# A four-layer graph network: tile 1's products ahead of tile 2's transposes where one layer hands its rows to the next, with the residuals' buffers first, divisions kept in order and the denominators' transfers later

## Chip, cores and metric

The kernel runs on one core of a Trainium2 chip as one program. The metric is the device time in microseconds (us), as the median of several runs. A core has five engines that work side by side, each through its own instructions in order: PE (matrix products and transposes), DVE (vector work), ACT (scalar functions, copies), POOL and SP (here mostly issuers of DMA transfers). They meet through semaphores.

## What is computed

There are 3327 nodes with 512 features. Four layers follow each other, and each is wrapped in a residual and a row-wise layer norm. The reference, cut to its form:

```
x = layernorm(x + attention8(x, adj, W0, a0))            # layer 0, 8 heads of 64
x = layernorm(x + sage(x, adj, Wn, bn, Wl, bl, 64))      # layer 1, the "maps"
x = layernorm(x + elu(attention8(x, adj, W2, a2)))       # layer 2
x = layernorm(x + elu(attention4(x, adj, W3, a3)))       # layer 3, 4 heads of 128

attention: Wh = x @ W
           e[i,j] = leaky_relu(s1[i] + s2[j], 0.2), masked by adj
           out[i] = sum_j softmax_j(e[i,j]) * Wh[j]
sage:      keep the first 64 neighbours of each row (by a running count)
           xj = leaky_relu(mean over kept X @ Wn.T + bn)
           xi = leaky_relu(X @ Wl.T + bl)
           out = xi + xj where a row has a neighbour
```

## The kernel before

Rows lie in 26 tiles of 128 (`NT` = 26, the last one padded). The 0/1 adjacency stays on the chip as one fp8 `mask`. An attention runs over two halves of 13 row tiles, and in each over four slots of heads. Per tile of neighbours DVE makes weights `t` (L405), PE multiplies them with the values (`po`, L428), ACT makes the fp8 part `y` of the denominators (L408), and PE sums it (`pd`, L380). At the end of a slot the sums `po` are copied to `ob`, transposed by PE, copied to `hb` by ACT (L465) and stored to the DRAM array `hd` by SP (L466). The denominators of the last slot of the second half go another way: DVE transposes `pd` (L497, L501), reduces it to `red` (L505), SP stores `dd` (L507), and 16 small loads (L517) bring it back as `pes` in the right places (`place`). `finish_sums` (L532 to L538) turns `pes` into the reciprocals `rec`. Both are left over in `self.late`, for the next layer to call.

**Finishing rows.** The layer after an attention reads `hd` again and finishes it two tiles at a time with `finish_steps`: `load` fetches the tile `h` from `hd` and its residual `xr` from the previous layer's input (L126; `xr` on POOL's queue, `h` on SP's, or on POOL's for the first pair), `divide` multiplies by `rec` (L181) and, where the layer has an ELU, takes an exponential `e` on ACT (L186), `add` adds the residual (L197, or L194 and L195), and `norm_rows` takes statistics (L152, L153), a square root on ACT (L154), a reciprocal (L155, L158) and scales the row on ACT (L161). The first two tiles, 0 and 1, are finished inside the end of the attention itself.

**The two passages.** Two places do so while PE takes the finished tiles into products:

- *The maps* (`sage`, layer 0 to layer 1). `step1` transposes a tile on PE (`pt`, L724) and copies it to `xT` on ACT (L726). `step2` multiplies it with two 512 x 512 weights on PE (`pz`, L732, and `pi`, L735; 16 matmuls with their weight loads), and ACT and DVE split `pz` into bf16 parts and finish `pi` with the bias and the row (L736 to L746). SP stores two results (L742, L747).
- *The third projection* (`third`, layer 2 to layer 3). `project1` transposes (L261, L262, and a row sum L263), `project2` multiplies (`pw`, L271) and makes the values `vt` (L272 to L277). SP stores the finished tile (L133) and the values (L283).

In both loops a tile's products are put off by one tile: in each turn the transposes of the new tile come first, then the products of the pending one:

```
for s, y in enumerate(ys):
    xT = step1(y)
    if s == 0 and t0 + 2 < NT:
        ahead = finish(...)          # the pair after this one
    if pend:
        step2(*pend)
    pend = (y, xT, t0 + s)
```

**What sets the order.** PE's order is the program's (`manual_schedule` for PE). All other engines' instructions, and the DMA issues on their queues, are ordered by a planner at build time, by program order among what it expects to be ready, with its own estimate of times. `keep_in_program_order(ins)` holds one instruction behind everything written earlier for its engine. A buffer that is used again waits for its last reader. A pool opened after another has closed lies on the same memory, and waits for the last use of those bytes; within a pool, buffers are laid out in the order in which their names are first asked for. Before the change the pool of the maps' rows holds 6 buffers of `h` and after them 2 of `xr`; that of the third projection 10 of `h` and 6 of `xr`.

Of the kernel before, what the change touches and what calls it, by code (L numbers as in the profile page):

```python
# [7 lines left out]
F32 = mybir.dt.float32  # L8
# [5 lines left out]
ALU = mybir.AluOpType  # L14
# [4 lines left out]
P = 128  # L19
# [13 lines left out]
def kernel(  # L33
# [10 lines left out]
    nc = tc.nc  # L44
    N, F = x.shape
# [66 lines left out]
    rec = const.tile([P, NT, 8], F32, name="rec")  # L112
# [52 lines left out]
    def finish_steps(pool, xin, layer, t0, n, hbufs=6, eng=nc.sync, xbufs=None, xpool=None, ebufs=None, pinned=False):  # L165
        H, D = layer.H, layer.D
        ys, xs, steps = [], [], []

        def load():
            for t in range(t0, t0 + n):  # L170
                h = pool.tile([P, F], F32, name="h", bufs=hbufs)
                load_tile(h, hd, t, eng)
                ys.append(h)
                xr = xpool.tile([P, F], F32, name="xr", tag="hb") if xpool else \
                    pool.tile([P, F], F32, name="xr", bufs=xbufs)
                load_tile(xr, xin, t, nc.gpsimd)
                xs.append(xr)

        def divide(s):
            h = ys[s]  # L180
            nc.vector.tensor_tensor(h.rearrange("p (h d) -> p h d", h=H), h.rearrange("p (h d) -> p h d", h=H),  # L181
                                    rec[:, t0 + s, :H].rearrange("p (h e) -> p h e", e=1).to_broadcast([P, H, D]),
                                    op=ALU.mult)
            if layer.elu:
                e = pool.tile([P, F], F32, name="e", bufs=ebufs)
                ins = nc.scalar.activation(e, h, AF.Exp)  # L186
                if pinned and s == 0:
                    tc.keep_in_program_order(ins)
                xs.append(e)

        def add(s):
            h, xr = ys[s], xs[s]
            if layer.elu:
                nc.vector.scalar_tensor_tensor(xr, xs[n + s], 1.0, xr, op0=ALU.min, op1=ALU.add)  # L194
                nc.vector.scalar_tensor_tensor(h, h, 0.0, xr, op0=ALU.max, op1=ALU.add)  # L195
            else:
                nc.vector.tensor_tensor(h, h, xr, op=ALU.add)  # L197

        steps.append(load)
        for s in range(n):  # L200
            steps += [lambda s=s: divide(s), lambda s=s: add(s)]
        steps.append(lambda: norm_rows(pool, ys, t0))
        return ys, steps

    def finish(*a):
        ys, steps = finish_steps(*a)
        for f in steps:
            f()
        return ys
# [476 lines left out]
    def sage(first, first_pool, xin, prev, nxt, wsrc, dst):  # L686
# [3 lines left out]
        with tc.tile_pool(name="sg_z", bufs=1, reuse_waits="tile") as zp, \  # L690
# [21 lines left out]
            with tc.tile_pool(name="sa_w", bufs=1, reuse_waits="tile") as wp, \  # L712
                    tc.tile_pool(name="sa", bufs=2, reuse_waits="tile") as fp, \
                    tc.tile_pool(name="sa_t", bufs=2, reuse_waits="tile") as sp, \
                    tc.tile_pool(name="sa_ps", bufs=2, space=PSUM, reuse_waits="tile") as ps:
                wn = load_w(wp, wnT, "wn", nc.gpsimd)
                wl = load_w(wp, wlT, "wl", nc.gpsimd)
                blb = wp.tile([P, F], F32, name="blb")
                nc.gpsimd.dma_start(out=blb, in_=bl.to_broadcast([P, F]))

                def step1(xt):
                    pt = ps.tile([P, FC, P], F32, name="pt")
                    for c in range(FC):
                        nc.tensor.transpose(pt[:, c, :], xt[:, c * P:(c + 1) * P], ident)  # L724
                    xT = sp.tile([P, FC, P], F32, name="xT")
                    nc.scalar.copy(xT, pt)  # L726
                    return xT

                def step2(xt, xT, t):
                    pz = ps.tile([P, F], F32, name="pz")  # L730
                    for c in range(FC):
                        nc.tensor.matmul(pz, xT[:, c, :], wn[:, c, :], start=c == 0, stop=c == FC - 1)  # L732
                    pi = ps.tile([P, F], F32, name="pi")
                    for c in range(FC):
                        nc.tensor.matmul(pi, xT[:, c, :], wl[:, c, :], start=c == 0, stop=c == FC - 1)  # L735
# [12 lines left out]


                cr = fp.tile([NT, P], BF, name="cr", bufs=1)  # L750
                nc.sync.dma_start(out=cr, in_=ctd[NT:NT + 1, :].rearrange("o (t p) -> (o t) p", p=P))
                cnt = zp.tile([P, 3, NT], F32, name="cnt")
                pend = None
                ahead = first
                for t0 in range(0, NT, 2):
                    ys = ahead
                    if t0 in (4, 8):
                        prev.late.pop(0)(fp)
                    if t0 == 8:
                        cf = fp.tile([NT, P], F32, name="cf", bufs=1)  # L760
                        nc.scalar.copy(cf, cr)
                        pt = ps.tile([P, FC, P], F32, name="pt")
                        cb = pt[:, 0, :NT]
                        nc.tensor.transpose(cb, cf, ident[:NT, :NT])
                        nc.vector.tensor_scalar(cnt[:, 0, :], cb, NEIGHBOURS, 1.0, op0=ALU.min, op1=ALU.max)
                        nc.vector.reciprocal(cnt[:, 1, :], cnt[:, 0, :])
                        nc.vector.tensor_scalar(cnt[:, 2, :], cb, 0.0, None, op0=ALU.is_gt)
                    for s, y in enumerate(ys):
                        xT = step1(y)
                        if s == 0 and t0 + 2 < NT:  # L770
                            ahead = finish(fp, xin, prev, t0 + 2, 2, 6, nc.sync if t0 else nc.gpsimd)
                        if pend:
                            step2(*pend)
                        pend = (y, xT, t0 + s)
                step2(*pend)
            first_pool.close()

            with tc.tile_pool(name="sb_w", bufs=1, reuse_waits="tile") as wp, \
# [8 lines left out]
                wsb = wp.tile([P, FC, 2, FW + nxt.H], F32, name="wsb")  # L787
# [104 lines left out]
    def third(first):  # L892
        with tc.tile_pool(name="col3", bufs=1) as cp, tc.tile_pool(name="at_r3", bufs=2, reuse_waits="tile") as rp:
# [3 lines left out]
            with tc.tile_pool(name="p_w", bufs=1, reuse_waits="tile") as wp, \  # L897
# [3 lines left out]
                wsb = wp.tile([P, FC, 2, FW + L3.H], F32, name="wsb")  # L901
# [5 lines left out]
                pend = None  # L907
                ahead = first
# [12 lines left out]
                for t0 in range(0, NT, 2):  # L921
                    ys = ahead
                    if t0 in (4, 8):
                        L2.late.pop(0)(fp)
                    load_group(t0 + 6)
                    for s, y in enumerate(ys):
                        t = t0 + s
                        store_tile(x3, y, t, nc.sync)
                        xT = L3.project1(pp, ps, y, t)
                        if s == 0 and groups:  # L930
                            ahead, steps = groups.pop(0)
                            for f in steps:
                                f()
                        if pend:
                            L3.project2(pp, bank, wsb, *pend)
                        pend = (xT, t)
                        if t == HALF + 1:
                            L3.prepare(pp, 0)
                            L3.first_rows = L3.rows(rp, 0, 0)
                            L3.cut(pp, 0)  # L940
                L3.project2(pp, bank, wsb, *pend)
                L3.mean(pp, bank, wsb)

# [133 lines left out]
    with tc.tile_pool(name="col0", bufs=1) as cp, tc.tile_pool(name="raw", bufs=2) as rawp, \  # L1077
# [4 lines left out]
        with tc.tile_pool(name="p_w", bufs=1, reuse_waits="tile") as wp, \  # L1082
# [37 lines left out]
            wsb = wp.tile([P, FC, 2, FW + L0.H], F32, name="wsb")  # L1120
# [104 lines left out]
```

## Time and profile before

| what | us |
|---|---|
| median of 3 runs | 3393.33 (3391.39 to 3394.57) |
| the profiled run's own time | 3389.15 |
| its span, first to last instruction | 3387.4 |
| PE busy | 3251.2 (96%) |
| DVE busy | 2687.5 (79%) |
| ACT busy | 2354.6 (70%) |
| mean PE clock granted | 0.985 |
| chain of waits: share of PE | 85% |
| passage into the maps | about 950 to 1170 |
| passage into the third projection | about 2544 to 2690 |

Times in the profile are microseconds from the span's start. A timeline line gives start, length, engine, the line of the kernel, operation, `output<-inputs`, the shape and in square brackets the idle time of that engine just before, with what ended it. A line of the waits gives who waited for whom, the total, how often, and the longest. "issue" stands where the profile shows no releaser. `SPq` and `POOLq` are the queues' own instructions.

### The profile page before, as it was taken

To read this page: it belongs to the slowest core of one execution; us is meant where nothing else is said; L and a number is where in the kernel's file an instruction comes from. 1 tells how busy PE (TensorE), PEld (TensorE's weight loads), DVE (VectorE), ACT (ScalarE), POOL (GpSimd) and SP (SyncE) were. 2 spreads that over 40 slices of the span, in tenths; PEclk is the share of its full clock that TensorE was granted. 3 is DMA by queue.
4 is the path that set the end of the run, shared out by engine and by line. 5 is a ranking of instruction groups with operands and counts; after the bars stand their busy time and mean duration, and the time that the engine had idled before them with its cause. 6 is when DMAs were issued, how large, how long until landed. Compare 5 with 4: busy or idle time off the path is not lost.

```text
span 3387.4 us, 47182 instructions
## 1 busy us (share of the span) xinstructions
PE 3251.2 (96%) x18476; PEld 1626.4 (48%) x18476; DVE 2687.5 (79%) x2619; ACT 2354.6 (70%) x2143; POOL 239.8 (7%) x389
## 2 busy tenths in 40 slices
PE   8899999999979999999989999999998999999997
PEld 7634344444434445545544444444446754455453
DVE  5799999999967544444449999999998766668887
ACT  2398998999953333333338999999997655558986
POOL 3100000000010011111110000000002000010110
PEclk9999999999999999999999999999998999999998
DMA  9644111110143343333320111111117411122211
GB/s 368 222 124 127 49 49 38 55 49 28 44 123 125 122 117 84 91 85 87 80 77 20 47 48 50 51 48 47 35 31 241 152 41 42 41 51 80 94 42 49
DMA packets 288014, 284.29 MB, mean 84 GB/s; under 512 B 107492, under 2 KB 223534, under 8 KB 287791
## 3 DMA queue, kind: packets, MB, share of 16 engines
q1 hardware_dynamic: 254063, 170.62, 16.6%
q0 software_dynamic: 28208, 102.96, 9.5%
q10 hardware_dynamic: 5520, 7.69, 0.7%
q8 instruction: 146, 2.39, 0.3%
q14 instruction: 77, 0.63, 0.1%
HBM read 212.01 MB, written 69.17 MB: 83 GB/s over the span
## 4 chain that ended last, share of the span: by engine, by line
PE 85%; DVE 5%; DMA 4%; ACT 3%; issue 2%; SPq 0%; ACTq 0%; DVEq 0%; POOL 0%; POOLq 0%
PE po L428 52%; PE acc L859 12%; PE pd L380 7%; PE pw L271 5%; DVE t L405 3%; PE pz L732 3%; DMA raw<-in_adjT_dram 3%; PE pi L735 3%; ACT y L408 1%; PE pt L456 1%; PE pk L819 1%; DMA h<-hd 0%; PE pa L1108 0%; PE pt L724 0%; PE pct L664 0%
## 5 line engine op out<-in xcount | busy, mean ns | idle before, releaser
L405 DVE SCALAR_TENSOR_TENSOR t<-rb,qc,mask 128x1664 f32<-128x1664 f32 x1040 | 1960.3, 1954 | 169.4 <-PE po L428 147.3
L408 ACT ACTIVATE y<-t,bi,sc 128x1664 fp8e4<-128x1664 f32 x1040 | 1769.5, 1766 | 310.4 <-PE pd L380 292.7
L428 PE MATMUL po<-t,vj 128*64 128x448 f32 (+3 forms) x8320 | 1909.6, 521 | 22.1 <-DVE t L405 19.6
L428 PEld LDWEIGHTS po<-t,vj 128*64 128x64 f32 (+1 forms) x8320 | 838.9, 148 | 970.6 <-issue 704.0
L859 PE MATMUL acc<-zs,kt 128*128 128x512 bf16 x1352 | 401.1, 380 | 0.0
L271 PE MATMUL pw<-wsb,xT 128*128 128x264 f32 (+1 forms) x1248 | 302.2, 397 | 15.2 <-DVE vt L277 12.0
L859 PEld LDWEIGHTS <-kt 128*128 128x128 fp8e4 x2002 | 196.1, 98 | 242.1 <-issue 7.7
L811 ACT CAST pk<-cy 128x512 f32<-128x512 bf16 x169 | 99.0, 588 | 277.4 <-DVE kt L823 266.3
L271 PEld LDWEIGHTS pw<-wsb,xT 128*128 128x128 f32 x1248 | 241.1, 197 | 60.7 <-ACT xT L262 10.8
L380 PE MATMUL pd<-y,sden 128*32 128x448 fp8e4 (+1 forms) x4160 | 259.5, 342 | 10.4 <-ACT y L408 10.4
L859 PE MATMUL acc<-zl,kt 128*128 128x512 bf16 x650 | 246.5, 379 | 0.0
L380 PEld LDWEIGHTS <-sden 128*32 128x32 bf16 x4160 | 117.5, 96 | 162.5 <-issue 139.8
L823 DVE SCALAR_TENSOR_TENSOR kt<-pk,mask 128x512 fp8e4<-128x512 f32 x169 | 116.1, 688 | 94.0 <-PE pk L819 94.0
L277 DVE TENSOR_TENSOR vt<-pw,dc 128x256 f32<-128x256 f32 x156 | 59.0, 418 | 148.2 <-ACT dc L272 143.7
L359 POOL DMA_DIRECT2D rb<-r x40 | 21.3, 532 | 1670.4 <-DVE t L405 1652.2
L275 ACT COPY rc<-pw 128x8 f32<-128x8 f32 (+1 forms) x78 | 12.6, 162 | 156.6 <-PE pw L271 154.1
L831 DVE SCALAR_TENSOR_TENSOR y<-acc,cnt,bnb 128x512 f32<-128x512 f32 x26 | 19.5, 751 | 97.7 <-PE acc L859 90.3
L732 PE MATMUL pz<-wn,xT 128*128 128x512 f32 x208 | 94.9, 600 | 1.7 <-ACT xT L726 1.7
L700 POOL DMA_DIRECT2D cy<-ctd x91 | 67.9, 746 | 385.1 <-ACT pk L811 312.6
L735 PE MATMUL pi<-wl,xT 128*128 128x512 f32 x208 | 93.5, 592 | 0.0
L634 DVE TENSOR_SCALAR mask<-raw 128x832 fp8e4<-128x832 int32 (+2 forms) x90 | 54.8, 614 | 38.9 <-DMA raw<-in_adjT_dram 38.5
L154 ACT ACT_TABLE_LOAD x45 | 57.7, 1283 | 37.0 <-DVE mv L153 36.4
(187 smaller groups left out, 1699.3 us busy)
## 6 DMA issues: line engine op xcount, KB each, us to landing
vj<-v SPq DMA_DIRECT2D x312, 128.0 KB
rb<-r POOLq DMA_DIRECT2D x40, 832.0 KB, 4.8
raw<-in_adjT_dram SPq DMA_DIRECT2D x67, 416.0 KB
cy<-ctd POOLq DMA_DIRECT2D x78, 256.0 KB, 4.0
h<-hd SPq DMA_DIRECT2D x61, 256.0 KB
v<-vt SPq DMA_DIRECT2D x50, 256.0 KB
hd<-hb SPq DMA_DIRECT2D x48, 256.0 KB
xr<-x POOLq DMA_DIRECT2D x45, 256.0 KB, 3.1
```

The costliest lines, as they stand in the source:

```text
L271: nc.tensor.matmul(pw[e][:, :FW + H], xT[:, c, :], wsb[:, c, e, :], start=c == 0, stop=c == FC - 1)
L277: nc.vector.tensor_tensor(vt[:, hs, :], pw[e][:, :FW].rearrange("p (h d) -> p h d", d=D), self.dc[:, t, hs].rearrange("p (h e) -> p h e", e=1)
L380: nc.tensor.matmul(pd[c][32 * kk:32 * kk + 32, :w_], lhsT, rhs, start=(kk, c) not in seen, skip_group_check=final is not None, stop=last a ...
L405: nc.vector.scalar_tensor_tensor(t, rb[k], self.qc[:, j, h:h + 1], mask[:, j, i0:i0 + IW], op0=ALU.max, op1=ALU.mult)
L408: nc.scalar.activation(y, t, AF.Sigmoid, bias=self.bi[:, j, h:h + 1], scale=self.sc[:, j, h:h + 1], saturate=False)
L428: nc.tensor.matmul(po[c][k * D:(k + 1) * D, :z - a_], vj[:, j % 2, k * D:(k + 1) * D], ts[k][:, a_:z], start=j == 0, stop=j == NT - 1)
L700: nc.gpsimd.dma_start(out=cy[:, :n, :], in_=ctd[t:t + n, b * GW:(b + 1) * GW] .rearrange("(o t) i -> o t i", o=1).to_broadcast([P, n, GW]))
L732: nc.tensor.matmul(pz, xT[:, c, :], wn[:, c, :], start=c == 0, stop=c == FC - 1)
L735: nc.tensor.matmul(pi, xT[:, c, :], wl[:, c, :], start=c == 0, stop=c == FC - 1)
L811: nc.scalar.copy(pks[k % 2], carry[b, t // 4 * 4][:, t % 4:t % 4 + 2, :])
L823: nc.vector.scalar_tensor_tensor(kt, pk, NEIGHBOURS, mask[:, t:t + 2, i0:i0 + GW], op0=ALU.is_le, op1=ALU.mult, saturate=False)
L859: nc.tensor.matmul(acc, kts[t][:, s * P:(s + 1) * P], zs(t, c) if c < 2 else zl[:, t, :], start=t == 0 and c == 0, stop=t == NT - 1 and c ...
```

## The change

Five edits are made.

1. In both passages the products of tile 1 are issued at the end of the first turn (`t0 == 0`), before the transposes of tile 2. From tile 2 on the lag of one tile is as before.
2. `finish_steps` asks for `xr` before `h`, so that in a pool that is new the residuals' buffers lie in front. The order of the loads stays.
3. With `pinned`, the divisions of all tiles of a pair are written ahead of the additions, and divisions of pairs after tile 2 are kept in program order. The maps now pass `pinned` for the pairs at tiles 2, 4 and 6; the third projection passes it, as before, for tile 2 alone.
4. The pinned exponential is named more narrowly: layer 2, pair at tile 2, first tile.
5. In the maps the two left-over steps of the denominators (`place`, `finish_sums`) come at `t0` 6 and 10 in place of 4 and 8.

```diff
@@ finish_steps
         def load():
             for t in range(t0, t0 + n):
+                xr = xpool.tile([P, F], F32, name="xr", tag="hb") if xpool else \
+                    pool.tile([P, F], F32, name="xr", bufs=xbufs)
                 h = pool.tile([P, F], F32, name="h", bufs=hbufs)
                 load_tile(h, hd, t, eng)
                 ys.append(h)
-                xr = xpool.tile([P, F], F32, name="xr", tag="hb") if xpool else \
-                    pool.tile([P, F], F32, name="xr", bufs=xbufs)
                 load_tile(xr, xin, t, nc.gpsimd)
                 xs.append(xr)
 
         def divide(s):
             h = ys[s]
-            nc.vector.tensor_tensor(...)
+            ins = nc.vector.tensor_tensor(...)
+            if pinned and t0 > 2:
+                tc.keep_in_program_order(ins)
             if layer.elu:
                 e = pool.tile([P, F], F32, name="e", bufs=ebufs)
                 ins = nc.scalar.activation(e, h, AF.Exp)
-                if pinned and s == 0:
+                if pinned and layer.li == 2 and (t0, s) == (2, 0):
                     tc.keep_in_program_order(ins)
                 xs.append(e)
...
         steps.append(load)
-        for s in range(n):
-            steps += [lambda s=s: divide(s), lambda s=s: add(s)]
+        if pinned:
+            steps += [lambda s=s: divide(s) for s in range(n)] + [lambda s=s: add(s) for s in range(n)]
+        else:
+            for s in range(n):
+                steps += [lambda s=s: divide(s), lambda s=s: add(s)]
@@ sage (the maps)
-                    if t0 in (4, 8):
+                    if t0 in (6, 10):
                         prev.late.pop(0)(fp)
...
                         if s == 0 and t0 + 2 < NT:
-                            ahead = finish(fp, xin, prev, t0 + 2, 2, 6, nc.sync if t0 else nc.gpsimd)
+                            ahead = finish(fp, xin, prev, t0 + 2, 2, 6, nc.sync if t0 else nc.gpsimd, None, None, None,
+                                           t0 < 6)
                         if pend:
                             step2(*pend)
                         pend = (y, xT, t0 + s)
+                    if t0 == 0:
+                        step2(*pend)
+                        pend = None
                 step2(*pend)
@@ third (the third projection)
                             L3.cut(pp, 0)
+                    if t0 == 0:
+                        L3.project2(pp, bank, wsb, *pend)
+                        pend = None
                 L3.project2(pp, bank, wsb, *pend)
```

More of the change, by code (lines that the diff above doesn't have):

```diff
@@ L180, in divide @@
             h = ys[s]
-            nc.vector.tensor_tensor(h.rearrange("p (h d) -> p h d", h=H), h.rearrange("p (h d) -> p h d", h=H),
-                                    rec[:, t0 + s, :H].rearrange("p (h e) -> p h e", e=1).to_broadcast([P, H, D]),
-                                    op=ALU.mult)
+            ins = nc.vector.tensor_tensor(h.rearrange("p (h d) -> p h d", h=H), h.rearrange("p (h d) -> p h d", h=H),
+                                          rec[:, t0 + s, :H].rearrange("p (h e) -> p h e", e=1).to_broadcast([P, H, D]),
+                                          op=ALU.mult)
+            if pinned and t0 > 2:
+                tc.keep_in_program_order(ins)
             if layer.elu:
```

## Prediction

> **What bounds the kernel now.** I read the page first (PE 96% busy, 85% of the chain), then the chain of waits, then waits and timeline where PE is not busy. The change touches two passages, in which an attention's end hands its rows to the next layer's matrix products: 950 to 1170 us (layer 0 to the maps) and 2544 to 2690 us (layer 2 to layer 3's projection). Chain of waits, first passage (start, length, what):
>
> ```profile
> 983.10 0.82 ACT h L161
> 983.97 1.11 PE pt L724 x4
> 985.08 4.62 PE pz L732 x8
> 989.70 3.43 PE pi L735 x8
> 993.13 0.44 PE pt L724 x4
> 993.57 3.44 PE pz L732 x8
> ...
> 1164.92 3.45 PE pi L735 x8
> ```
>
> From 983.97 on only PE is on the chain, a tile every 7.31 us (0.44 transposes, 6.87 products), until 1168.37; ahead of it stands ACT's normalising of tile 2. So this stage ends when it starts plus its PE work. The timeline shows the start:
>
> ```profile
> 959.26 0.55 POOL L126 DMA_DIRECT2D h<-hd  x1
> 967.63 0.69 DVE L181 TENSOR_TENSOR h<-h,rec 128x512 f32<-128x512 f32 x1 [5.85 <-DMA h<-hd]
> 969.73 0.54 POOL L126 DMA_DIRECT2D xr<-in_x_dram  x1 [9.92 <-issue]
> 972.85 0.69 DVE L197 TENSOR_TENSOR h<-h,xr 128x512 f32<-128x512 f32 x1 [4.53 <-DMA xr<-in_x_dram]
> 977.21 0.69 DVE L181 TENSOR_TENSOR h<-h,rec 128x512 f32<-128x512 f32 x1 [2.25 <-DMA h<-hd]
> 983.97 1.11 PE L724 MATMUL pt<-ident,h 128*128 128x128 f32 x4 [13.84 <-ACT h L161]
> ```
>
> PE ends tile 0's products at 970.13 and stands 13.84 us with tile 1's xT ready: its order puts tile 2's transposes ahead of tile 1's products. Tile 2 is late because POOL stood 9.92 us before its residual xr, with tile 3's h and xr queued behind. In the compiled program before, that xr lies at byte 200,960 of a partition, over the last `hb` of the attention, whose store leaves SP near 962.8. DVE then held a division of tile 4 (977.21) ahead of tile 3's addition.
>
> Second passage, waits for 2565 to 2574 and busy times by stretch (length, PE, PEld, DVE, ACT, POOL, clock, DMA share, GB/s):
>
> ```profile
> PE pt L261 <- ACT h L161: 8.5, 1, 8.5
> ```
>
> ```profile
> 2565.00:2574.00 9.00, 0.54 (x4) 0.49 (x4) 8.97 (x21) 6.25 (x11) 2.35 (x5) 0.65 0.76 204
> 2574.00:2594.00 20.00, 20.00 (x92) 17.13 (x92) 18.16 (x42) 16.35 (x33) 3.06 (x6) 0.90 0.83 267
> 2594.00:2614.00 20.00, 19.02 (x96) 16.23 (x96) 18.49 (x44) 14.57 (x34) 1.77 (x4) 1.00 0.80 259
> 2614.00:2635.00 21.00, 16.06 (x85) 13.35 (x84) 20.07 (x60) 17.37 (x40) 2.69 (x5) 1.00 0.68 225
> 2635.00:2680.00 45.00, 45.00 (x224) 38.75 (x222) 31.70 (x79) 29.59 (x70) 1.06 (x2) 0.96 0.50 173
> ```
>
> The same wait, 8.46 us, but DVE is busy 65.7 of 70 us up to 2635: the supply of rows bounds this passage nearly as much as PE. I therefore price the two differently.
>
> **What the Trainium skill says.** "TensorE: Matmul & The Clock Gate", "What's actually happening": after an idle window of about 3.4 us the clock is halved until as much sustained work. The trace agrees: 1.11 and 4.62 us after the gap for 0.44 and 3.44. The same page, "Architectural detail": ACT and DVE are strictly first in, first out; DVE's wait at 977.21 fits. "DMA: Bandwidth & Descriptors", "Anatomy of one DMA": some 2.0 us fixed plus bytes / 436 GB/s, 2.6 us for 256 KB; the trace has 2.9 to 3.4 us alone and 8.3 us for tile 2's h behind the 1 MB `wl`. "ScalarE: Activation LUTs", "What ACT_TABLE_LOAD costs": 1283 ns, which the trace has too, and a drain of 1380 ns that it doesn't show: the square root starts at once after its load.
>
> **The change, part by part.**
>
> *Tile 1's products ahead (maps).* The 16 matmuls move from 985.08 to 970.13 and end at 977.0. Nothing is added. Tile 2's transposes, SP and POOL are not behind them in any queue; the five DVE operations (L738 to L746) and two ACT casts that follow move along.
>
> *Residuals in front (maps).* The two xr slots take the pool's lowest addresses: xr2 the very bytes of h2 before (188,672), into which its load went at once at 959.26, xr3 those of another `y` that PE last reads by 958.3. POOL then issues xr2, h3, xr3 at 959.8, 960.4, 960.9 (0.54 us each) instead of 969.7 to 970.8. They land behind `wl` (957.98 + 6.3 us) and h2 (967.6): at 250 to 324 GB/s about 1 us apiece, so xr3 near 971, an estimate. The new owner of byte 200,960 is tile 4's h, on SP: it can be issued from 969.7, before it was at 972.89. DVE does two divisions, two additions, two statistics for tiles 2 and 3 (0.69 us each) and two aggregates (0.17): done at 972.5 if nothing is between, at 976.0 if tile 0's five operations (3.45 us) are. From there to a normalised tile 2: square root 0.29, reciprocal 0.17, product 0.16, scaling 0.81 and gaps, 2.0 us; 3.4 us with DVE as busy as before. Tile 2 is ready between 974.5 and 979.4, PE at 977.0. Tile 3's scaling (0.7), xT's copy (0.6) and gaps (0.3) put the products of tile 2 between 977.9 (PE's own transposes) and 981.0. I take 979.2. From there 24 x 6.87 + 22 x 0.437 + 0.17 = 174.7 us, and 0.5 for tile 4: end 1154.4 against 1168.37, **14.0 us saved** (bounds 11.7 to 15.8). The clock's loss (0.67 + 1.18 us) is in it, as PE stands too briefly.
>
> *Divisions in order.* For tiles 4 to 7 of layer 0 they stay behind the DVE work written before, for tile 4 the last operation of tile 1 (PE 977.0, then 3 x 0.69: 979.3). Behind it wait tile 4's and 5's additions and statistics; tile 4 is ready 5.3 us on, 984.6, and PE wants it at 979.2 + 6.87 = 986.1. Tile 6's division stands behind tile 2's last operation, 988.2, ready 993.5, wanted near 1000.7. Cover: one product. If PE were early, 1 us (in the bounds).
>
> *Denominators later.* The 16 small DMAs (L517, near 0.61 us each on SP) and DVE's L532 to L538 (about 1.5 us) go two tiles' pairs back. On SP h4 to h7 pass ahead of 15 of them (before, six stood ahead of h4 and 15 of h6); behind them may come h8's load. That costs at most 16 x 0.61 = 9.8 us of queue near 1003, of which tile 8, wanted near 1015.3 and needing 3 us to land and 5.3 on DVE and ACT, feels 0 to 5.8: I take 0, as the load is free to go earlier (its slot is tile 2's, done at 988.2); 5.8 would make the forecast 3384.1, inside the range. Their reader is tile 13's division, two pairs of tiles on.
>
> *Second passage.* Tile 1's 16 products move to 2565.1 and end at 2569 to 2570.5. The wait for tile 2 (2573.5) is then 3 to 4.5 us; with the clock halved, tile 2's products begin near 2575.6 and end at 2581 against 2583.63. But tile 6 is ready at 2590.55 and was used at 2591.55: about 1 us of lead passes, and ACT's copies (0.98 us at 2601, 1.30 at 2618) and `rr` (3.64 at 2635) come next. The new layout here puts tile 3's h in the slot that held xr3: POOL's 1.1 us wait for PE moves one place up, h3 issues 1.6 us and the two `wsb` loads 0.55 us later; tile 3's division (2556.28) and product 0 (2559.27) are covered by the later wait. Divisions ahead of additions for tiles 2 and 3: they ran so already. **1 us saved**, bounds 2 lost to 4 saved, since the order of ACT and DVE is planned anew.
>
> *At nothing.* The exponential's new condition names the one instruction pinned before, as the group of layer 2 is pinned at tile 2 alone. In layer 3's attention xr was the first asked for already; in the attentions' endings it comes from another pool.
>
> **Sum.** 14.0 + 1.0 = 15.0: span 3387.4 to 3372.4, profiled run 3389.15 to 3374.2. The median of the runs, 3393.33, lies 4.2 above that run; the forecast is on it: **3378.3 us**.
>
> **Rivals.**
> 1. *Only the product fills the gap (9%).* Something else late holds xr2, or DVE's order keeps tile 2 at 983.97. Then two tiles' transposes and a copy stand bare, and the halved clock falls on tile 2: products begin at 986.6 and cost 1.2 more, against 993.57: 5.8 us saved, and nothing in the second passage: 3387.5. For it: the profile names no engine for the 9.92 us, only "issue". Against: bytes and store match.
> 2. *The second passage follows PE (12%).* If ACT and DVE, which waited 3.9 and 0.9 us for PE after 2574, move up with it, the lead of 2.6 to 4.3 us lasts: 18 us saved in all, 3375. Against: DVE at 94%.
> 3. *Slower (5%).* A pinned division waits on DVE for a load late on SP. Place: tile 4's h behind the last `hb` store and whatever of L517 still floats ahead of it. 15 of those end near 978.5, h4 lands by 983, tile 4 is ready 5.3 us later against 986.1: 2 us of PE. The sign turns only if h4 lands after 995.8 (5.3 more, less 986.1, is 15.0), and it is over 0.2% after 1002.6, 40 us from the store at 962.8: then 3401. The longest landing of a row load in this passage was 8.3 us.
>
> **How the numbers follow.** Main case 74%, own range 3373.5 to 3383.6 (gains 9.7 to 19.8). With the runs' scatter of 1.6 either way and most of rival 2, and towards rival 1, the range is 3372 to 3386. A measurement tells 0.2%, 6.8 us, from no change: faster 0.86 (main, rival 2), same 0.09 (rival 1), slower 0.05.
>
> **What would show it.** POOL's xr2 within 1 us of h2; tile 1's `pz` straight after tile 0's `pi`; the wait of L724 on L161 under 3 us; `pz` at 3.4 us from tile 2 on; the last `pi` near 1154. Then stages keep their length until 2530; the second passage's wait near 4 us, and its end earlier than the shift by about 1 us. Wrong: xr2 still after 969; a DVE wait of several us before L181 of tile 4; L517 ahead of h8 with a PE gap near 1015; the second passage longer.

## The result and the profile after

| | before | after |
|---|---|---|
| median of 6 runs, us | 3390.98 (3386.04 to 3394.57) | 3377.49 (3376.60 to 3378.99) |
| ratio of the runs | | 0.9961, 95% interval 0.9950 to 0.9972 |
| profiled execution, its span | 3389.15, 3387.4 | 3378.99, 3377.3 |
| passage into the maps: first division (L181) to the end of the last `pi` | 219.98 | 211.76 |
| passage into the third projection: first division to the start of the last `pw` | 139.76 | 136.09 |

The change made the kernel about 13.5 us faster by the medians, and the forecast, 3378.3, is met. The two passages gave other amounts than forecast, though: the maps 8.2 us in place of 14.0, the third projection 3.7 in place of 1.0. From here on a passage is measured from its own first division, so that shifts from earlier work stay out; each length is that of one profile. All later line numbers are those of the kernel after: in the maps L724, L726, L732, L735, L738 are now L729, L731, L737, L740, L743, and the casts that were L736 and L739 are L741 and L744. The span's difference in this one pair of profiles, 10.1 us, is 1.2 before the maps, 8.2 in them, 3.7 in the second passage, less 1.4 in the stage of the maps that follows and 2.0 in the second attention, and 0.3 in the rest. The profiled run of before lies 1.8 us below its median and that of after 1.5 above.

In the chain of waits of after (start, length, what) PE is alone from 990.75 on, with tile 3's products at 991.41. Ahead of that the chain still goes through ACT's normalising and back to DVE; the line at 977.89 is tile 3's, the one at 989.88 tile 4's:

```profile
977.89 0.80 ACT h L161
...
989.88 0.82 ACT h L161
990.75 0.66 PE pt L729 x4
991.41 3.44 PE pz L737 x8
994.84 3.43 PE pi L740 x8
...
1155.46 3.45 PE pi L740 x8
```

Tile 2's normalising starts at 977.17; before it was 983.10, which is 4.7 us later on the passage's own clock. Tile 2's first product takes 5.79 us where a tile later takes 3.44. PE's timeline of after shows what lies between (start, length, line, operation, in brackets the idle time before and what ended it):

```profile
972.16 3.60 PE L740 MATMUL pi<-wl,xT 128*128 128x512 f32 x8
978.04 1.82 PE L729 MATMUL pt<-ident,h 128*128 128x128 f32 x8 [2.28 <-ACT h L161]
981.08 5.77 PE L737 MATMUL pz<-wn,xT 128*128 128x512 f32 x8 [1.21 <-ACT xT L731]
986.69 3.60 PE L740 MATMUL pi<-wl,xT 128*128 128x512 f32 x8
```

Tile 1's products follow tile 0's without a gap, and the 13.84 us of waiting became 2.28 + 1.21. The second of these ends with the copy of tile 2's xT, which ACT makes at 980.45, behind its two casts for tile 1. Waiting is not all that is lost: transposes of 1.82 us and a first product of 5.77 say that PE's clock is down. The stretches of after, cut at these events, give it (length, busy PE, PEld, DVE, ACT, POOL, then granted clock, DMA share, GB/s):

```profile
975.60:978.00 2.40, 0.16 (x1) 0.00 (x0) 1.47 (x4) 0.83 (x2) 0.00 (x0) 1.00 0.95 311
978.00:979.90 1.90, 1.82 (x8) 1.14 (x8) 0.69 (x1) 1.16 (x2) 0.00 (x0) 0.62 0.93 281
979.90:981.10 1.20, 0.02 (x1) 0.03 (x1) 0.53 (x1) 1.18 (x3) 0.00 (x0) 0.50 0.34 19
981.10:984.50 3.40, 3.40 (x4) 1.49 (x5) 3.33 (x7) 0.41 (x1) 0.00 (x0) 0.50 0.60 192
```

The other forecast event is there: the residuals leave POOL right behind their rows (timeline of after, for tile 2; its residual was at 969.73 before).

```profile
958.02 0.55 POOL L126 DMA_DIRECT2D h<-hd  x1
958.57 0.54 POOL L126 DMA_DIRECT2D xr<-in_x_dram  x1
```

So why is tile 2 still late? DVE's timeline of after:

```profile
972.14 0.69 DVE L743 TENSOR_TENSOR r<-pz,zs 128x512 f32<-128x512 f32 x1 [3.16 <-ACT zs L741]
972.75 0.68 DVE L199 TENSOR_TENSOR h<-h,xr 128x512 f32<-128x512 f32 x1
```

DVE stands for 3.16 us at tile 0's subtraction `r`, with tile 3's addition behind it. It waits for ACT's cast `zs`, although `pz` of tile 0 ended near 965.3. ACT's timeline of after says why:

```profile
971.31 0.30 ACT L766 CAST cf<-cr 26x128 f32<-26x128 bf16 x1 [9.11 <-DMA cr<-ctd]
971.52 0.59 ACT L741 CAST zs<-pz 128x512 bf16<-128x512 f32 x1
```

A cast of 0.30 us, `cf`, which takes 26 counts of neighbours and is written in the turn of tile 8, was put ahead of the cast of tile 0. It waits 9.11 us for its load. In the profile of before it stood there too (970.03, 6.60 us of waiting for the same load), but there tile 2 was later for other reasons.

In the second passage the wait for tile 2 fell from 8.46 to 4.37 us, and new waits for tiles 4, 10 and 12 came: 2.00, 1.55 and 0.67. Further on, where PE transposes coefficients of the attention (`pr`) and waits for ACT's copy of it (`rr`), a wait of before got shorter. PE's timeline of before, and below it that of after:

```profile
2573.51 1.12 PE L261 MATMUL pt<-ident,h 128*128 128x128 f32 x4 [8.46 <-ACT h L161]
2574.42 5.42 PE L271 MATMUL pw<-wsb,xT 128*128 128x260 f32 x16
...
2634.75 0.75 PE L312 MATMUL pr<-ident,rc 128*4 128x128 f32 x5 [3.64 <-ACT rr L314]
...
2635.77 5.36 PE L271 MATMUL pw<-wsb,xT 128*128 128x260 f32 x16
```

```profile
2567.78 1.97 PE L266 MATMUL pt<-ident,h 128*128 128x128 f32 x8 [4.37 <-ACT h L161]
2569.58 5.19 PE L276 MATMUL pw<-wsb,xT 128*128 128x260 f32 x16
2576.77 0.66 PE L266 MATMUL pt<-ident,h 128*128 128x128 f32 x4 [2.00 <-ACT h L161]
...
2625.75 0.75 PE L317 MATMUL pr<-ident,rc 128*4 128x128 f32 x5 [1.21 <-ACT rr L319]
...
2626.78 3.67 PE L276 MATMUL pw<-wsb,xT 128*128 128x260 f32 x16
```

The product behind the wait for tile 2 is slow in both kernels. The one behind the wait for `rr` is slow in before alone. ACT copies `rr` 4.05 us after its transposes began in before (2634.13), behind two table loads and two normalisings, and 1.64 us after them in after (2625.14).

### The profile page after: what moved, and what is told of

The parts are those of the page before. It is cut to its first block, busy times and chain, and to the rows that moved or that the text cites. A ratio compares the mean times of both kernels' runs of the same rounds, so it can differ in the third digit from the quotient of the medians.

```text
span 3377.3 us, 47143 instructions
## 1 busy us (share of the span) xinstructions
PE 3252.0 (96%) x18424; PEld 1627.4 (48%) x18476; DVE 2687.1 (80%) x2619; ACT 2358.2 (70%) x2145; POOL 239.6 (7%) x389
## 4 chain that ended last, share of the span: by engine, by line
PE 81%; DVE 5%; DMA 5%; issue 5%; ACT 4%; POOL 0%; SPq 0%; POOLq 0%; DVEq 0%; ACTq 0%
PE po L433 49%; PE acc L869 12%; PE pd L385 7%; PE pw L276 4%; DMA raw<-in_adjT_dram 3%; DVE t L410 3%; PE pz L737 3%; PE pi L740 2%; ACT y L413 1%; PE pk L829 1%; PE pt L461 1%; DMA h<-hd 1%; PE pa L1122 0%; DMA dd<-red 0%; PE pct L669 0%
## 5 line engine op out<-in xcount | busy, mean ns | idle before, releaser
L869 PE MATMUL acc<-zs,kt 128*128 128x512 bf16 x1312 | 393.8, 381 | 2.2 <-issue 0.2
L737 PE MATMUL pz<-wn,xT 128*128 128x512 f32 x208 | 95.8, 604 | 1.6 <-ACT xT L731 1.6
L740 PE MATMUL pi<-wl,xT 128*128 128x512 f32 x208 | 93.5, 592 | 0.0
```

The lines of the kernel that those rows point to most:

```text
L869: nc.tensor.matmul(acc, kts[t][:, s * P:(s + 1) * P], zs(t, c) if c < 2 else zl[:, t, :], start=t == 0 and c == 0, stop=t == NT - 1 and c ...
```

## Experiments

Two theories of mine, and their rivals. **Late arrivals in a row:** tile 2 becomes ready when the last of four things is done: its residual's landing, the division of tile 4 that stands before tile 3's addition, the cast `cf` that stands before tile 0's, and then PE's own order. Each edit takes one away and uncovers the next, so single edits bring little and the sum more. **PE's clock:** the short waits and transposes ahead of tile 2 halve it, and some 2 to 3 us of the passage are that. Rivals: the product alone carries the gain; the buffers carry it; the second passage gains from a shift, not from its own edit.

The measured values; each ratio is to runs of before on the same chip, and the passages are of one profile each:

| kernel | median us (runs) | ratio, 95% interval | maps | tile 2's scaling, us after first division | third |
|---|---|---|---|---|---|
| before | 3390.98 (6) | 1 | 219.98 | 34.72 | 139.76 |
| after | 3377.49 (6) | 0.9961 (0.9950 to 0.9972) | 211.76 | 30.03 | 136.09 |
| e1_product_alone | 3387.05 (20) | 0.9988 (0.9982 to 0.9995) | 217.26 | 34.86 | 138.07 |
| e2_maps_product_back | 3384.58 (10) | 0.9979 (0.9969 to 0.9988) | 216.61 | 31.43 | 135.63 |
| e3_residuals_behind | 3382.27 (7) | 0.9974 (0.9964 to 0.9985) | 212.81 | 31.73 | 135.95 |
| e4_cf_in_order | 3372.11 (5) | 0.9947 (0.9935 to 0.9960) | 207.99 | 26.91 | 136.08 |
| e5_third_product_back | 3383.60 (20) | 0.9980 (0.9974 to 0.9987) | 212.49 | 30.04 | 140.37 |
| e6_divisions_free | 3384.37 (13) | 0.9984 (0.9976 to 0.9993) | 217.83 | 35.91 | 136.02 |
| e7_denominators_early | 3377.72 (5) | 0.9964 (0.9951 to 0.9977) | 211.92 | 30.07 | 135.75 |
| e8_busy_pe | 3375.79 (4) | 0.9954 (0.9939 to 0.9969) | 209.72 | 30.00 | 136.66 |
| e9_no_pin | 3384.30 (14) | 0.9981 (0.9973 to 0.9989) | 217.59 | 36.01 | 136.18 |
| e10_residuals_behind | 3380.03 (6) | 0.9970 (0.9959 to 0.9981) | 213.89 | 31.58 | 135.73 |
| e11_early_pair | 3381.09 (6) | 0.9974 (0.9962 to 0.9985) | 212.56 | 30.85 | 135.85 |
| e12_busy_third | 3371.98 (5) | 0.9954 (0.9941 to 0.9967) | 208.01 | 26.91 | 135.70 |

How far a passage's length can be trusted is seen where two kernels have the same maps: e4 and e12 take 207.99 and 208.01, after and e5 211.76 and 212.49. So in the maps a difference below about 1 us in one pair of profiles shows nothing. In the third projection before and e1 have the same code and differ by 1.7 us; the eleven kernels with the edit there lie between 135.6 and 136.7, the three without it between 138.1 and 140.4. The time ahead of the maps, with no edit in it, goes from 945.1 to 952.2 us in these profiles, so the medians are the coarser measure.

**e1, the product alone.** Before, with the one edit in the maps:

```diff
+                    if t0 == 0:
+                        step2(*pend)
+                        pend = None
                 step2(*pend)
```

> The kernel before, with one edit alone: the products of tile 1 ahead of the transposes of tile 2 in the maps. Theory A (two causes: the product fills the gap, and the freed buffer makes tile 2 early): POOL still stands some 10 us before the residual of tile 2, tile 2 is ready near 983, PE waits about 7 us for it after tile 1's products, the clock is halved behind it; 5 to 6 us less than before, and nothing in the second passage: near 3385.3. Theory B (the product alone did it, the buffers do nothing): the passage is 8.2 us shorter as after the change, near 3382.8.

2.7 us in the passage, half of what theory A forecast, and the time is 3387.05. DVE's timeline of e1 has both delays of before:

```profile
971.95 0.69 DVE L197 TENSOR_TENSOR h<-h,xr 128x512 f32<-128x512 f32 x1 [4.86 <-DMA xr<-in_x_dram]
...
976.22 0.69 DVE L181 TENSOR_TENSOR h<-h,rec 128x512 f32<-128x512 f32 x1 [2.17 <-DMA h<-hd]
```

The product fills part of the gap, but the gap ends when it ended before (tile 2's scaling 34.86 us after the first division, 34.72 before), with PE's clock down (tile 2's first product 6.78 us). The product alone gives a third of the passage's gain.

**e2, all but the product in the maps.** After, with these three lines taken out.

> The changed kernel, with tile 1's products in the maps put back behind tile 2's transposes. Theory A: tile 2 is early all the same (ready 977 to 978 of the span), PE waits some 8 us from the end of tile 0's products, and the maps' passage keeps 3.5 to 5.5 us of its 8.2: 2.7 to 4.7 us slower than the changed kernel, near 3381. Theory B: all 8.2 us are gone, near 3385.7.

The passage is 3.4 us shorter than before, just under theory A's 3.5 to 5.5. Together with e1's 2.7 this makes 6.1, where both together gave 8.2: PE's order and the supply of tile 2 are worth more together than apart, as a path needs. The comparison is not clean, though. The held division of tile 4 is now written ahead of tile 1's work on DVE, and it stands between the two halves of tile 2's reciprocal, so that tile 2's scaling comes 1.4 us later than in after:

```profile
980.04 0.69 DVE L181 TENSOR_TENSOR h<-h,rec 128x512 f32<-128x512 f32 x1 [0.75 <-issue]
980.65 0.15 DVE L158 SCALAR_TENSOR_TENSOR rs<-mv,rs 128x2 f32<-128x2 f32 x1
```

**e3, residuals behind.** After, with `xr` asked for after `h` again:

```diff
-                xr = ...
                 h = pool.tile([P, F], F32, name="h", bufs=hbufs)
                 load_tile(h, hd, t, eng)
                 ys.append(h)
+                xr = ...
                 load_tile(xr, xin, t, nc.gpsimd)
```

> The changed kernel, with xr asked for after h again (the buffers' old layout in both passages). Theory A: POOL stands 9 to 10 us before tile 2's xr, tile 2 is ready near 982, the passage loses 2 to 3 us of its 8.2; the second passage within 1 us: near 3380. Theory B: no change, 3377.5.

The residual of tile 2 is again issued 21.3 us after the first division in place of 11.4, but the passage is only 1.05 us longer, hardly more than two profiles of the same maps differ. The edit that the prediction took for the heart of the matter shows next to nothing here; e10 will show that `cf` hides it, since with `cf` in ACT's way tile 3's addition is late in any case.

**e4, the cast `cf` held in program order.** After, with one word more:

```diff
-                        nc.scalar.copy(cf, cr)
+                        tc.keep_in_program_order(nc.scalar.copy(cf, cr))
```

> The changed kernel with one ACT instruction kept in program order: the cast of cr to cf (L766), which in the changed kernel stands 9.1 us on ACT for its DMA, ahead of the first cast of pz. No other engine's order changes. Theory C (what is left of PE's wait comes from ACT: cf holds the cast, the cast holds DVE's subtraction 3.2 us, that holds tile 3's addition and both tiles' scaling, and PE's clock is halved behind it): tile 2 ready by 975.5, PE's wait on L161 under 0.5 us, pz of tile 2 at 3.4 to 3.8 instead of 5.8 us: 4.5 to 6.5 us faster than the changed kernel, near 3372. Theory D (tile 3's addition waited for its residual's transfer, cf only filled the time): less than 1 us.

DVE's order is unchanged, and on ACT this one instruction moves (to 1013.38). The cast of tile 0 starts at 963.96, as soon as its product is there, tile 2's scaling 3.1 us sooner after the first division, and the passage is 3.8 us shorter than after. PE's timeline of e4:

```profile
970.62 3.60 PE L740 MATMUL pi<-wl,xT 128*128 128x512 f32 x8
974.06 1.04 PE L729 MATMUL pt<-ident,h 128*128 128x128 f32 x8
976.43 3.70 PE L737 MATMUL pz<-wn,xT 128*128 128x512 f32 x8 [1.33 <-ACT xT L731]
...
985.47 0.66 PE L729 MATMUL pt<-ident,h 128*128 128x128 f32 x4 [1.91 <-ACT h L161]
```

No wait is left ahead of tile 2's transposes, and the clock stays up (1.04 and 3.70). The last line is the next late arrival: tile 4. The passage gains less than the 4.5 us forecast, the median 5.4. The maps of e4 and e12, 208.0 both, are shorter than those of after and e5 (211.8 and 212.5) by far more than the scatter, while the intervals of the ratios of e4 and after overlap.

**e9 and e10, two edits taken back with `cf` out of the way.** Both are e4; e9 has the divisions free again (the two added lines of `divide` out), e10 the residuals behind.

> As e4_cf_in_order, but the divisions of the pairs at tiles 4 and 6 are not held in program order. With the cast still free (e6_divisions_free) that cost 6 us in the maps' passage, as the planner put tile 4's division, which waits for a load on SP, ahead of tile 3's addition. Theory that the two early placements are independent: the passage grows from 208.0 by about 6 to 214 and the time to about 3378. Rival, that with the cast out of the way the planner has no hole in which to put the division: the passage stays at 208 to 209 and the time near 3372.

> As e4_cf_in_order, but xr is again asked for after h, so that its buffers lie behind and POOL issues it some 10 us later (21.3 in place of 11.4 after the passage's first division). The orders of all five queues are those of e4. In e3_residuals_behind, with the cast still in the way, this cost 1.05 us of the maps' passage and tile 2 was 1.7 us later. Theory that the cast hid most of what the buffers in front are worth: xr of tile 3 now lands near 25.5, its addition runs at 25.5 instead of 22.5, tile 2's scaling starts near 30 instead of 26.9, PE waits 2 us at a falling clock, the passage grows by 3 to 5 us to 211 to 213, time 3375 to 3377. Rival, that the front buffers matter little in any case: 1 us, 3373.

The passage is 9.6 us longer in e9, more than the 6 forecast, and 5.9 longer in e10, just above its forecast; in e10 the orders of all five queues are those of e4. So the buffers in front are worth 5.9 us where nothing else is late and 1.05 where `cf` is. DVE's timeline of e10:

```profile
970.34 0.69 DVE L199 TENSOR_TENSOR h<-h,xr 128x512 f32<-128x512 f32 x1 [5.46 <-DMA xr<-in_x_dram]
```

**e6, the divisions free.** After, without

```diff
-            if pinned and t0 > 2:
-                tc.keep_in_program_order(ins)
```

> The changed kernel without the two lines that keep the divisions of tiles 4 to 7 in program order. DVE's plan then has the division of tile 4 ahead of the addition of tile 3 again. Theory F (this order, more than the buffers, made tile 2 early): DVE stands for tile 4's h, tile 2's scaling starts at 33 to 35 us after the passage's first division instead of 30.0, the maps' passage takes 214 to 217 us instead of 211.8: near 3381. Theory A as predicted (the buffers made tile 2 early): within 1 us of the changed kernel.

6.1 us longer than after. DVE's timeline, and below it SP's:

```profile
979.41 0.69 DVE L181 TENSOR_TENSOR h<-h,rec 128x512 f32<-128x512 f32 x1 [8.23 <-issue]
980.01 0.68 DVE L197 TENSOR_TENSOR h<-h,xr 128x512 f32<-128x512 f32 x1
```

```profile
972.43 3.85 SPq L520 DMA_DIRECT2D pes<-dd  x6
976.33 2.02 SPq L126 DMA_DIRECT2D h<-hd  x4
```

(Behind L181 the line numbers of e6 are two lower than those of after.) The planner put tile 4's division ahead of tile 3's addition. DVE stands 8.23 us there ("issue": the profile names no releaser), and the division starts 3.1 us after SP issued tile 4's row, as it does in e11 below. SP held that row behind six small loads of the denominators, which wait for `dd`. Tile 3's addition follows at once; in after, with the same loads, it ran 5.1 us sooner on the passage's own clock. e6 and e9 agree (217.83 and 217.59): with the division in front, it no longer matters whether `cf` is late. Nor do product and buffers together give more here than the product alone (e1, 217.26). What was taken back is the hold on the division; that the divisions of a pair are written ahead of the additions, the other half of edit 3, was not taken back alone.

**e7, the denominators early.** After, with `t0 in (4, 8)`.

> The changed kernel with the denominators' two steps at tiles 4 and 8 again. DVE's plan of the first tiles stays. My prediction: nothing, within 1 us in the maps' passage. Rival (the 15 small loads ahead of tile 6 and 7 on SP cost): 2 us or more slower, with a PE wait at tile 6.

Nothing: 3377.72, and the passage is 0.2 us longer, within the scatter. In both kernels six of the sixteen small loads stand ahead of tile 4's row on SP.

**e8, PE kept busy.** After, with ten products of the fp8 mask on PE after tile 1's, and five more between tile 3's transposes and tile 2's products; nobody reads their results.

```diff
+                def busy(k):
+                    pb = qp.tile([P, 4 * P], F32, name="pb", tag="q")
+                    for _ in range(k):
+                        nc.tensor.matmul(pb, upto, mask[:, 0:2, :2 * P], start=True, stop=True)
...
+                        if (t0, s) == (2, 1):
+                            busy(5)
...
+                        busy(10)
```

> The changed kernel with 10 extra matmuls (128x512 bf16 x fp8, about 0.22 us each, result unused) after tile 1's products and 5 more after tile 3's transposes, where PE stands. They take no time from the rest. Theory G (transposes don't count as work for PE's clock, so that 2.3 us of wait, 1.8 of transposes and 1.2 of wait add up to an idle window): transposes at 1.0 instead of 1.8 us, tile 2's pz at 3.6 to 3.8 instead of 5.8: 2 to 3 us faster in the passage, 208.8 to 209.8 us. Rival (the clock falls for another reason): no gain or up to 1 us lost.

PE's timeline of e8:

```profile
973.93 2.32 PE L758 MATMUL pb<-mask,upto 128*128 128x512 fp8e4 x10
976.36 1.36 PE L729 MATMUL pt<-ident,h 128*128 128x128 f32 x8
977.56 1.24 PE L758 MATMUL pb<-mask,upto 128*128 128x512 fp8e4 x5
979.40 3.70 PE L737 MATMUL pz<-wn,xT 128*128 128x512 f32 x8 [0.59 <-ACT xT L731]
```

Tile 2's first product begins 33.9 us after the first division in both kernels, and takes 3.70 here against 5.77. The passage is 2.04 us shorter, with work added. That is the theory of the clock, at its size; the intervals of the two ratios overlap, so the medians, 3375.79 and 3377.49, agree in sign only.

**e5, the product of the third projection back.** After, without the three lines in `third`.

> The changed kernel with tile 1's products in the third projection put back behind tile 2's transposes. From the last divisions of layer 2's attention to the last pw this passage took 139.8 us before and 136.1 after. Theory A (the product gave it, the rest of PE, ACT and DVE moved up with it): back to 138.5 to 139.8, 2.4 to 3.7 us slower than the changed kernel. Theory E (the new plan of ACT and DVE and the buffers gave it): within 1 us of 136.1.

The passage grows by 4.3 us, a little more than forecast, the median by 6. PE's waits for tile 2 and for `rr` in e5:

```profile
2568.89 1.12 PE L266 MATMUL pt<-ident,h 128*128 128x128 f32 x4 [7.64 <-ACT h L161]
...
2630.41 0.75 PE L317 MATMUL pr<-ident,rc 128*4 128x128 f32 x5 [3.42 <-ACT rr L319]
```

The second passage's gain is its own edit's, not a shift from the first. The wait for `rr` goes with it: 3.4 to 3.6 us in the three kernels without this edit, 1.2 in all eleven with it. The buffers have no part in it: with them behind (e3) the passage takes 135.95 us, after 136.09.

**e12, PE kept busy in the third projection.** e4, with ten products after tile 1's there, results unread:

```diff
                         L3.project2(pp, bank, wsb, *pend)
                         pend = None
+                        pb = bank(0)
+                        for _ in range(10):
+                            nc.tensor.matmul(pb, mask[:, 0, :P], mask[:, 0, :512], start=True, stop=True)
```

> As e4_cf_in_order, and in the passage into the third projection ten matmuls whose result nobody reads run on PE after tile 1's products, while PE would wait for tile 2 (4.42 us in e4). They take 2.3 us at the full clock. In e4 the clock falls there to 0.50 and tile 2's 16 products take 5.13 us against 3.67 for a later tile, its transposes 1.97 against 1.2; then PE waits 2.00 us for tile 4. Theory that PE's clock sets this passage: tile 2's transposes and products end 2.0 us earlier, and so does the passage (136.1 to about 134.1), time near 3370. Theory that the supply of rows by DVE and ACT sets it, as with tile 4's wait: the 2.0 us come back as a longer wait for tile 4 (2.0 to about 4.0), the passage keeps 136.1 within 0.5 and the time 3372.

PE's timeline of e12:

```profile
2566.16 2.32 PE L957 MATMUL pw<-mask 128*128 128x512 fp8e4 x10 [0.87 <-DVE vt L282]
2569.94 1.36 PE L266 MATMUL pt<-ident,h 128*128 128x128 f32 x8 [1.47 <-ACT h L161]
2571.28 3.77 PE L276 MATMUL pw<-wsb,xT 128*128 128x260 f32 x16
2577.05 0.66 PE L266 MATMUL pt<-ident,h 128*128 128x128 f32 x4 [2.00 <-ACT h L161]
2577.54 5.36 PE L276 MATMUL pw<-wsb,xT 128*128 128x260 f32 x16
```

Tile 2's products take 3.77 us in place of 5.13, as expected of the clock. Yet the passage is 135.70 us against 136.08 in e4. The wait for tile 4 did not grow, as the expectation of the supply had it: tile 4 came 1.7 us sooner too (36.95 us after the passage's first division, 38.61 in e4). Tile 3's products are slow instead, 5.36 against 3.67, for after the 2.00 us the clock fell, where in e4 it did not. The stretches behind that wait, of e12 and then of e4:

```profile
2579.00:2580.50 1.50, 1.50 (x5) 1.11 (x5) 1.50 (x5) 1.48 (x2) 0.00 (x0) 0.50 0.83 224
2569.20:2573.00 3.80, 3.77 (x19) 3.35 (x20) 3.72 (x8) 3.77 (x7) 0.00 (x0) 1.00 1.04 373
```

Tile 5's transposes begin 42.64 us after the passage's first division here and 42.62 in e4. So the gain is lost at once, but neither theory named how. The profiled run of e12 is one of two of its five near 3380, the others near 3371.6; its extra time against e4 lies before the maps (6.6 us) and in the stage after them (3.1), where e12 has no edit, and its cause stays open.

**e11, the pair of tiles 4 and 5 written earlier.** e4, with `finish` for that pair ahead of tile 1's products:

```diff
+                        early = finish(fp, xin, prev, 4, 2, 6, nc.sync, None, None, None, True)
                         step2(*pend)
                         pend = None
```

> As e4_cf_in_order (its one ACT cast held in order), and the pair of tiles 4 and 5 is written ahead of tile 1's products in place of after them, so that the held division of tile 4 stands on DVE before tile 1's five operations and no longer behind them. In e4 that division ran at 978.58 although its row had landed, PE waited 1.91 us for tile 4 and ACT 0.83. Theory of head of line (what stands first in DVE's order and waits, or comes later than it could, is what is left of the passage): tile 4 is ready 3 to 4 us earlier, the 1.91 us go, the maps' passage falls from 208.0 to about 206.2, the time by 1 to 2 us from e4's 3372.1 to about 3370.5. Rival, by which the division's place is right and holding it early makes DVE wait for tile 4's load with tile 1's work queued behind: the passage grows by up to 3 us, near 3375.

My theory fell and the rival holds, further than it said: 4.6 us longer than e4. DVE's and SP's timelines of e11:

```profile
976.87 0.69 DVE L181 TENSOR_TENSOR h<-h,rec 128x512 f32<-128x512 f32 x1 [3.50 <-issue]
977.48 0.15 DVE L158 SCALAR_TENSOR_TENSOR rs<-mv,rs 128x2 f32<-128x2 f32 x1
```

```profile
969.91 3.86 SPq L522 DMA_DIRECT2D pes<-dd  x6
973.82 2.02 SPq L126 DMA_DIRECT2D h<-hd  x4
```

The held division now stands 3.50 us and starts 3.05 us after SP issued tile 4's row. Queued right behind it is the second half of tile 2's reciprocal, 0.15 us of work that ACT's scaling needs. A held order is right only where the data are there: of the two places tried, the one that the change chose, behind tile 1's work, is the better.

## Why the prediction was right, and where it was not

- **What bounds the maps' passage** held: a wait ahead of tile 2, then PE at 7.3 us a tile. From tile 3 on the products of after take 3.44 and 3.43.
- **Tile 1's products ahead** held to the letter. Rival 1, that only this would work, was priced at 5.8 us; the product alone (e1) gives 2.7 in its passage. Its tile 2 products begin at 986.39, 0.9 us later than priced on before's clock, and take 3.3 us more than at the full clock, where 1.2 was priced.
- **Residuals in front**: the cause was right. POOL issues `xr` 0.55 us after `h`, and 5.9 us hang on it once `cf` is out of the way (e10). The step that failed is "I take 979.2" for tile 2's products. On before's clock (after's first division is 1.24 us earlier) tile 2 was ready at 979.3, at the late end of the bounds, and its products began at 982.3, outside them: 3.1 us of the 5.8 that are missing; 2.3 more are the first product at the low clock. The last `pi` ended at 1160.1 on that clock, where 1154.4 was forecast. The step counted DVE's work on tiles 2 and 3 and perhaps tile 0's, but not that DVE would wait for ACT. What stood in the way was `cf`, in the list of groups of before with 6.6 us of idle time ahead of 0.3 us of work. In before something longer covered it, and the prediction passed over it. The skill's sentence that it cited, on ACT and DVE as strictly first in, first out ("TensorE: Matmul & The Clock Gate", "Architectural detail"), holds for this cast as well: 9.11 us on ACT and 3.16 behind it on DVE. Where a stall is to be removed, the stalls beneath it are the next bound. With `cf` held (e4) the passage is 12.0 us shorter than before, inside the bounds of 11.7 to 15.8.
- **"The clock's loss is in it, as PE stands too briefly"** failed. From tile 0's products on, no wait in the passage of after is longer than 2.28 us, and the clock fell to 0.50; e8 measures the loss at 2.0 us. The Trainium skill's "TensorE: Matmul & The Clock Gate", "Part 4: PE-mode transpose", says that a transpose does not count as a busy PE in the way that a product does. After and e8 fit that: from the end of tile 1's products at 975.6 to 981.1 PE had only transposes, 5.5 us, and with fp8 products put in between the clock stayed at 1.00. That it is the transposes and not the sum of two short waits was not separated.
- **Divisions in order** was mis-sized. The prediction worked out their cover and booked no gain of their own, although it had named the held-up addition at 977.21. Letting them free again costs 6.1 us (e6), or 9.6 with `cf` out of the way (e9): it is the edit on which the gain of the buffers rests.
- **Denominators at 0** held (e7). Its detail did not: six of the small loads still stand ahead of tile 4's row, not one, and in e11 the held division waits for that row. That the row would be in time without them was not tried.
- **Second passage, 1.0 us, bounds −2 to +4**: 3.7 came, in the upper part of the bounds. The lead was given back, as said: 4.1 us less at tile 2, 4.2 more at tiles 4, 10 and 12. Tile 13's products begin 1.1 us earlier than before on the passage's own clock, which is what was priced; by tile 15's it is 4.6. The failed step is "ACT's copies (0.98 us at 2601, 1.30 at 2618) and `rr` (3.64 at 2635) come next": in the new order PE has no wait for those copies, its wait for `rr` is 1.21 us, and the product behind that takes 3.67 us in place of 5.36. Rival 2, by which the lead lasts and 18 us are saved in all, did not come. What it gave for this passage, 2.6 to 4.3 us, came by another way.
- **The sum**: the two wrong terms are −8.2 for −14.0 and −3.7 for −1.0, so 11.9 for 15.0. The profiled run was to take 3374.2 and took 3378.99. The gain by medians is 13.5. That the forecast still fell within 1 us of the median is partly luck: it was set on 3393.33, the median of three runs, and the six runs of before have 3390.98, so that an anchor 2.4 us too high met a gain 1.5 us too large.

## What to carry to other kernels

Before pricing the removal of a stall, list every instruction that waits at the same time on an engine that works strictly in order, even one of 0.3 us: what lies under the stall is the next bound, and an edit that is worth 6 us alone in the way may show 1 us until the last of them is gone. To judge the edits of a bundle, take each one back from the best version, not only from the full change. Hold an order by hand where the planner puts an operation on a late load ahead of one that is ready, and only there.

## What the runs showed of the hardware

- PE's granted clock fell to 0.50 with no wait above 2.28 us (after, 975.6 to 981.1), and in e12 after a wait of 2.00 us; in e4 a wait of 2.00 us at the same place left it at 1.00. In these traces the length of a single wait does not decide it; what does was not found.
- Fifteen fp8 products, ten of 2.32 us and five of 1.24 us together, read by nobody, made the maps' passage 2.04 us shorter (e8). In the third projection ten of them only moved the slow products from tile 2 to tile 3 (e12: 3.77 for 5.13 us, then 5.36 for 3.67).
- A 0.30 us cast cost the passage 3.8 us by its place in ACT's queue (e4), and a change of buffer addresses alone, with all five queues in the same order, 5.9 us (e10).
